# The second scan's end for tokens 512 to 1023, placed behind the first chunk of the ternary feed-forward

## The chip, the cores and the metric

The kernel runs on one core of a Trainium2 chip. The metric is the device time of one execution in microseconds (us). The profile names the core's engines: PE (TensorE: matmuls and transposes), DVE (VectorE), ACT (ScalarE), POOL (GpSimd), and SP (SyncE), whose queue issues most of the transfers (DMAs). Each engine works through its own instructions in order.

## The reference, cut to what matters

Activations `x` are [1024 tokens, 256 features] in float32 (4 sequences of 256). Eight residual blocks follow one another, each on a layer norm of `x`:

```
x += tanh(g) * scan0(ctx, LN(x))        # state-space scan over ctx, gated by silu(LN(x))
x += tanh(g) * mixture0(LN(x))          # 16 experts, top 4, and a shared one
x += tanh(g) * scan1(ctx, LN(x))        # the second scan
x += tanh(g) * ffn1(LN(x))              # ternary weights
x += tanh(g) * attention2(LN(x), ctx)   # 32 heads, rotated keys and queries
x += tanh(g) * ffn2(LN(x))
x += tanh(g) * attention3(LN(x), ctx)
x += tanh(g) * mixture3(LN(x))
```

A scan's state-space part depends on `ctx` alone: `y = scan(ctx) + D*u`. Only its end depends on `x`:

```
y = y * silu(z)        # z = LN(x), x after mixture0
x = x + tanh(g) * y^T
```

The ternary feed-forward is

```
gate, up = split(LN(x) @ Wgu^T)         # 1024 hidden units each
h = silu(gate) * up
x = x + tanh(g) * (h * rsqrt(mean(h*h) + eps)) @ Wp^T
```

It mixes features of one token, never two tokens.

## The kernel before, in words

All of `x` stays in on-chip memory as `x[128, 8 tiles, 256]`. A tile is 128 tokens, and a half `h` is four tiles: half 0 is tokens 0 to 511, half 1 is tokens 512 to 1023. `xn` has the same shape and holds the layer norm that is in use, half by half.

**Order of work.** The kernel is written as a straight program over tiles. A planner then sets each engine's order by readiness and by place in the program; an instruction inside `keep_in_program_order` is kept behind what was written before it for its engine. `pinned_turn` is a PE transpose of that kind, and `silu_z` keeps its two ACT activations that way. The memory of a pool that was closed goes to pools opened later, and their first use waits until the old pool's tiles are done with.

**Second scan and first mixture.** `s1 = Scan(1, ...)` computes the scan's state-space part beside the mixture's blocks (`beside`). The outcome lies in `du` ([128, 2, 1024] float32, 8 KB in each partition), beside `u`, `delta` and others in the pool `ssm1`. When the blocks are done, the mixture's end loads each token's four expert results from DRAM (`y<-y_d`, L969, sixteen transfers of 256 KB through four buffers) and adds them to `x` tile by tile (L981 on DVE; for every third tile ACT L978 and POOL L979). After each tile it calls `hook("done", t)`. After tile 3 and after tile 7, `beside` makes that half's layer norm (stats L179, `rs_r` L186 on POOL, `ln_m` L190, the normed tiles L195 and L198), the gate `silu_z` (L451 on ACT) and `finish`: two DVE products `du<-du,xn` (L459), eight PE transposes in four `yt_ps` tiles (the helper's line, L577), four updates of `x` (L464).

**Ternary feed-forward** (`ffn1`). It makes both halves' layer norms and turns them with `transpose_half2` (eight transposes `xt_ps` a half, L222; high part by ACT L224, rest by DVE L225). Then `chunk(h, c)` runs for two halves of eight chunks of 128 hidden units: eight matmuls into `g_ps` and `u_ps` (L1068), ACT's silu `sg` (L1073), the DVE product `hh` (L1075), its split `hp` (L1077, L1078), its square (L1080 or L1083) and, on POOL, the sum of squares (L1084). `results(h)` multiplies with the second weight matrix (L1104, L1108). [...]the stage takes two as `pt` (tag "tp": `xt_ps` and small things) and six for `g_ps`, `u_ps` and `o_ps`.

**Beside it, the attention's start** (`Heads`, opened just before `ffn1`): it loads `wa` (768 KB, L1168) and `pos` (8 KB, L1173), makes sines and cosines on DVE and ACT (L1177 to L1193), clears `v` on POOL (L1212, L1213), and `first(h, c)` puts the first keys, values and queries between chunks. Its memory is that of the scan's closed pools.

Of the kernel before, what the change touches and what calls it, by code (L numbers as in the profile page):

```python
# [12 lines left out]
F32 = mybir.dt.float32  # L13
# [8 lines left out]
P = 128  # L22
# [3 lines left out]
NT = B * L  # L26
T = NT // P
H2 = 512
# [24 lines left out]
def tile_kernel(ctx: ExitStack, tc: tile.TileContext, a: dict, out: bass.AP):  # L53
# [35 lines left out]
    rows = const.tile([P, 536], F32, name="rows")  # L89
# [80 lines left out]
    def layer_norm_half(h, split=True):  # L170
        for _ in layer_norm_steps(h, nc.vector, nc.scalar, nc.gpsimd, split):
            pass
# [44 lines left out]
    def transpose_half2(pool, h, hi, lo):  # L217

        for k in range(2):
            ps = pool.tile([P, 4, P], F32, name="xt_ps", tag="tp")  # L220
            for i in range(4):
                nc.tensor.transpose(ps[:, i, :], xn[:, h * 4 + i, k * P : (k + 1) * P], ident)  # L222
            pf = ps.rearrange("p i q -> p (i q)")
            nc.scalar.copy(hi[:, k, :], pf)  # L224
            nc.vector.tensor_tensor(lo[:, k, :], pf, hi[:, k, :], ALU.subtract)  # L225
# [5 lines left out]
    class InOrder:  # L231
        def __init__(self, engine):
            self.engine = engine
# [14 lines left out]
    class Scan:  # L248


        def __init__(self, li, es, width, rows, squares, mm):
            self.li, self.mm = li, mm
            self.w, self.wr, self.pr = ssm_w[li], ssm_r[li], ssm_p[li]
            sp = es.enter_context(tc.tile_pool(name=f"ssm{li}", bufs=1))
            self.rot = es.enter_context(tc.tile_pool(name=f"ssm{li}r", bufs=2))
            self.work = es.enter_context(tc.tile_pool(name=f"ssm{li}w", bufs=1))
            dr = es.enter_context(tc.tile_pool(name=f"ssm{li}d", bufs=1, space=bass.MemoryType.DRAM))
            self.width, self.rows, self.squares = width, rows, squares
            self.u = sp.tile([P, 2, NT], F32, name="u")
            self.delta = sp.tile([P, 2, NT], F32, name="delta")  # L260
            self.du = sp.tile([P, 2, NT], F32, name="du")
            self.bcp = sp.tile([96, NT], BF16, name="bcp")
            self.an = sp.tile([P, 2, NS], F32, name="an")
            self.b_dram = dr.tile([NS, NT], F32, name="b_dram")
# [781 lines left out]

    def ffn1(gate, guT, prT, beside):
        with ExitStack() as es:  # L1050
            fp = es.enter_context(tc.tile_pool(name="ffn1", bufs=1))
            fr = es.enter_context(tc.tile_pool(name="ffn1r", bufs=2))
            pt = es.enter_context(tc.tile_pool(name="ffn1t", bufs=2, space=PSUM))
            pg = es.enter_context(tc.tile_pool(name="ffn1g", bufs=2, space=PSUM))
            xps = [[fp.tile([P, 2, H2], F32R, name=f"xp{h}{i}") for i in range(2)] for h in range(2)]
            s2 = [fp.tile([P, H2], F32, name=f"s2{h}") for h in range(2)]
            for h in range(2):
                layer_norm_half(h)
                transpose_half2(pt, h, *xps[h])
            hps, invs = {}, {}  # L1060

            def chunk(h, c):
# [48 lines left out]

            for h in range(2):
                for c in range(8):
                    chunk(h, c)
                    if h == 1 and c == 1:
                        scales(0)
                        results(0)
                    beside(h, c, pt)
# [520 lines left out]
    def g(i):  # L1639
        return tg[:, i : i + 1]  # L1640

    with ExitStack() as es:
        dr = es.enter_context(tc.tile_pool(name="terd", bufs=1, space=bass.MemoryType.DRAM))
        slab_d = [dr.tile([P, 1024], BF16, name=f"slab{i}") for i in range(6)]
# [53 lines left out]
        for h in range(2):  # L1698
            s0.finish(h, g(0), bank, pinned_turn)
        ea.close()  # L1700
        s1 = Scan(1, es, H2, 5, 2, pinned_mm)
        ep = ExitStack()
        kept = {}
        steps = s1.scan(pq, [((dt,), h * H2, H2) for h in range(2) for dt in range(2)], shared=4, c_banks=("c", "c1"), ahead=1)
# [2 lines left out]
        turned = {}  # L1707

        def beside(name, n):
            def step():  # L1710
                if len(made) in (15, 23):
                    widths.append(s1.softplus(len(widths), 1))
                if widths:
                    next(widths[-1], None)
                made.append(next(steps, None))

            if name == "start":
                kept["pre"] = pre = ep.enter_context(tc.tile_pool(name="ssm1pre", bufs=1, side="right"))
                kept["taps"] = s1.taps(pre)
                kept["bc"] = pre.tile([104, NT], F32, name="bc")  # L1720
                s1.decay()
                s1.convolved_by_taps(0, [s1.wide(pq, f"dA{dt}") for dt in range(2)], kept["taps"])
            elif name in ("tables", "pairs"):
                h = int(name == "pairs")
                if h:
                    s1.convolved_by_taps(1, [s1.wide(pq, f"dA{dt}") for dt in range(2)], kept["taps"])
                s1.rows_bc(h, s1.wide(pq, "c"), kept["pre"], kept["bc"])
                for dt in range(2):
                    s1.steps_dt(dt, h, s1.wide(pq, ("y0", "dA1")[dt]), kept["bc"])
                if h:  # L1730
                    s1.ready(pq)
                    ep.close()
                else:
                    for dt in range(2):
                        for _ in s1.softplus(dt, 0):
                            pass
            elif name in ("part", "block"):
                for _ in range(0 if n < 0 else 1 if name == "part" else 2 + (n in (7, 14))):
                    if len(made) < 65:
                        step()  # L1740
            elif name == "branch":
                while len(made) < 65:
                    step()
            elif name == "blocks":
                ew.close()
                tern = et.enter_context(tc.tile_pool(name="wtern", bufs=1, side="right"))
                turned["gu"] = tern.tile([P, 2, 2048], F32R, name="guT")
                turned["pr"] = tern.tile([P, 8, 256], F32R, name="prT")
                yp = es.enter_context(tc.tile_pool(name="moe0y", bufs=1, side="right"))
                ternary_turned(yp, bank, slab_d, turned["gu"], turned["pr"], pinned_turn)  # L1750
                return yp
            elif name == "done" and n % 4 == 3:
                h = n // 4
                layer_norm_half(h)
                s1.silu_z(h)
                s1.finish(h, g(1), bank, pinned_turn)

        mixture(0, g(4), 4, P, weights, route0, weights0, (ph, po, pt), beside, by_tanh=True, G=2)
    eh = ExitStack()
# [3 lines left out]
        heads.bank = lambda shape, dtype, name: pt.tile(shape, dtype, name=name, tag="tp")  # L1763
        heads.first(h, c)

    ffn1(g(5), turned["gu"], turned["pr"], first)
    et.close()
    with tc.tile_pool(name="wfp8", bufs=1, side="right") as w8:
        wq = w8.tile([P, 4608], F32R, name="wq8")
        cols = w8.tile([P, 12], F32, name="cols")  # L1770
        nc.sync.dma_start(out=cols, in_=a["scales2"])
        with tc.tile_pool(name="quant", bufs=1, side="right") as qp:
            xattn2(g(2), heads, Rounding(qp, wq, a["ffn2"]))
        eh.close()
        with tc.tile_pool(name="att3", bufs=1, side="right") as a3:
            attT = a3.tile([P, B, 2, L], F32, name="attT")
            ffn2(g(6), wq, cols, attT)
            xattn3(g(3), attT)
# [106 lines left out]
```

## Time and profile before

| | us |
|---|---|
| median of 3 runs | 979.47 |
| lowest and highest of them | 969.01, 979.48 |
| profiled execution, its own time | 963.2 |
| its span, first to last instruction | 961.5 |
| PE busy | 738.9 (77%) |
| DVE busy | 714.7 (74%) |
| ACT busy | 451.5 (47%) |
| POOL busy | 472.1 (49%) |
| sums of expert results (L981), first start and end of the last | 461.1 to 481.2 |
| first and last matmul of `g_ps` and `u_ps` in the ternary feed-forward, starts | 493.5 to 546.0 |
| its last matmul `o_ps` (L1104), start | 564.0 |

All places in time are counted from the span's first instruction, in the profiled execution. "Busy" leaves out the issuing of transfers. A row such as `DVE x L981 x2` in a chain means two such instructions one after another; in a timeline row, what stands in brackets is how long the engine was idle before it and what ended that. A busy engine in one stage says nothing about another stage, so the text below reads stage by stage. PEclk is PE's granted clock as a share of full speed.

### The profile page before, as it was taken

Reading aid. Unit: us, or ns where it says so; the run is one execution under the profiler, and the core shown is the slowest. Engines: PE = TensorE matmul, PEld = TensorE weight load, DVE = VectorE, ACT = ScalarE, POOL = GpSimd, SP = SyncE. Lnnn points to the kernel's source line nnn. Section 1 sums busy time; section 2 is a strip of 40 time slices with the busy share of each in tenths; the row PEclk is TensorE's granted clock in tenths of the full one; section 3 lists DMA queues with packets and bytes.
Section 4 is the critical chain, followed back from the end, with each engine's and each line's share of the span. In section 5 each row is a group of like instructions: output and inputs, shape, how many; then the busy total and the mean of one; then the engine's idle time right before and its main releaser. Section 6 shows DMA issues by size and latency. Waiting matters only on the chain.

```text
span 961.5 us, 12035 instructions
## 1 busy us (share of the span) xinstructions
PE 738.9 (77%) x3736; PEld 457.3 (48%) x3736; DVE 714.7 (74%) x1406; ACT 451.5 (47%) x875; POOL 472.1 (49%) x432
## 2 busy tenths in 40 slices
PE   5454657669599889896268879989999896989991
PEld 1121222225356555463247756655655675655550
DVE  6998989985989999997787568788775587362332
ACT  4565664513345555353545517666666472102331
POOL 1575685631068878884337524646420332006642
PEclk8586677898679999899579968888869999798996
DMA  4564553301225436573610020000000006603224
GB/s 135 197 231 148 186 179 122 120 1 44 57 78 176 142 117 176 167 177 92 204 34 1 0 99 2 1 2 1 1 2 1 6 1 260 194 4 90 88 67 148
DMA packets 43490, 90.17 MB, mean 94 GB/s; under 512 B 6208, under 2 KB 17360, under 8 KB 43248
## 3 DMA queue, kind: packets, MB, share of 16 engines
q1 hardware_dynamic: 36416, 71.01, 23.2%
q0 software_dynamic: 6144, 16.79, 5.9%
q10 hardware_dynamic: 864, 1.57, 0.4%
q8 instruction: 32, 0.52, 0.2%
q14 instruction: 34, 0.28, 0.1%
HBM read 76.10 MB, written 13.24 MB: 93 GB/s over the span
## 4 chain that ended last, share of the span: by engine, by line
PE 30%; DVE 9%; ACT 4%; DMA 4%; POOL 3%; issue 2%; SPq 0%; DVEq 0%; ACTq 0%; POOLq 0%
PE h_ps L574 5%; PE o_ps L574 3%; PE av_ps L1337 3%; PE sa L1337 2%; DVE gm L239 2%; DMA y<-y_d 2%; PE sb L1337 2%; DMA y_d<-o_sb,place 1%; PE o_ps L1104 1%; DVE m L239 1%; PE o_ps L1558 1%; PE m_ps L1340 1%; PE g_ps L1536 1%; PE h_t_ps L577 1%; PE u_ps L1536 1%
## 5 line engine op out<-in xcount | busy, mean ns | idle before, releaser
L239 DVE TENSOR_TENSOR_SCAN st<-dA,dBu 128x512 f32<-128x512 f32 (+1 forms) x112 | 153.1, 1368 | 4.0 <-ACT dA L239 2.5
L239 POOL TENSOR_TENSOR dBu<-du,b_sb 128x512 f32<-128x512 f32 (+1 forms) x96 | 142.4, 1497 | 20.2 <-DVE st L239 19.2
L239 ACT ACTIVATE dA<-delta,an 128x510 f32<-128x510 f32 (+1 forms) x112 | 83.3, 747 | 126.1 <-DVE st L239 108.2
L239 DVE TENSOR_REDUCE gm<-sa 128x2 f32<-128x512 f32 x128 | 82.0, 683 | 19.8 <-PE sa L1337 19.2
L785 POOL DMA_INDIRECT xg<-xn_d,token x64 | 63.7, 996 | 64.4 <-PE o_ps L574 45.8
L239 DVE TENSOR_TENSOR yc<-st,c 128x512 f32<-128x512 f32 (+1 forms) x112 | 85.6, 764 | 13.0 <-PE c L430 1.7
L430 PE MATMUL c<-bcp,c_selC 96*128 96x512 bf16 x64 | 28.2, 484 | 75.4 <-DVE yc L239 75.3
L239 ACT ACTIVATE ex<-sb 128x512 f32<-128x512 f32 x128 | 69.7, 598 | 34.3 <-PE sb L1337 34.0
L409 PE MATMUL y<-yc,ident 128*128 128x512 f32 x128 | 84.1, 766 | 2.1 <-DVE yc L239 1.2
L871 POOL DMA_INDIRECT y_d<-o_sb,place x64 | 65.9, 1030 | 36.2 <-ACT hT L239 17.0
L409 PEld LDWEIGHTS y<-yc,ident 128*128 128x128 f32 x128 | 31.6, 248 | 88.9 <-issue 70.3
L574 PE MATMUL y<-yc,ident 128*128 128x512 f32 x128 | 68.4, 616 | 2.0 <-DVE yc L239 0.9
L186 POOL TENSOR_TENSOR rs_r<-ln_v,half 128x4 f32<-128x4 f32 x14 | 14.9, 1064 | 100.0 <-DVE ln_v L184 91.0
L1337 PE MATMUL sa<-kT,qT 32*128 32x256 f32 x256 | 42.6, 378 | 8.3 <-DVE gm L239 7.7
L1337 PE MATMUL sb<-qT,kT 32*128 32x256 f32 x256 | 48.2, 363 | 0.1
L1337 PE MATMUL av_ps<-ex,v 128*32 128x256 f32 x512 | 41.8, 445 | 0.6 <-DVE mx L239 0.2
L574 PE MATMUL h_ps<-w0a,xgT 128*128 x160 | 41.5, 406 | 0.7 <-issue 0.7
L239 POOL TENSOR_TENSOR du<-delta,u 128x512 f32<-128x512 f32 x8 | 10.9, 1365 | 63.3 <-DVE delta L239 62.3
L574 PEld LDWEIGHTS y<-yc,ident 128*128 128x128 f32 x128 | 24.8, 196 | 36.1 <-issue 23.0
L1337 PE MATMUL sb<-mxT,onesr 32*128 32x256 f32 x256 | 40.1, 306 | 0.0
L638 ACT ACTIVATE sg<-h_ps 128x176 f32<-128x176 f32 (+1 forms) x30 | 11.2, 374 | 59.2 <-PE h_ps L574 55.4
L639 DVE TENSOR_TENSOR hh<-sg,h_ps 128x176 f32<-128x176 f32 (+1 forms) x44 | 16.5, 376 | 26.3 <-ACT sg L638 16.5
(382 smaller groups left out, 1870.6 us busy)
## 6 DMA issues: line engine op xcount, KB each, us to landing
b_sb<-b_dram SPq DMA_DIRECT2D x32, 512.0 KB
b_sb<-b_dram SPq DMA_DIRECT2D x64, 256.0 KB
w3a<-in_moe3a SPq DMA_DIRECT2D x16, 480.0 KB
w0a<-in_moe0a SPq DMA_DIRECT2D x16, 384.0 KB
y<-y_d SPq DMA_DIRECT2D x24, 256.0 KB
wf<-in_ffn SPq DMA_DIRECT2D x6, 512.0 KB
wf<-in_ffn SPq DMA_DIRECT2D x3, 768.0 KB
xn_d<-xn SPq DMA_DIRECT2D x8, 256.0 KB
```

The costliest lines, as they stand in the source:

```text
L186: pool.tensor_tensor(r, v, half[:, 0:4], ALU.pow)
L239: ins = f(*args, **kw)
L409: self.mm(y_ps[:, q : q + H2], lhsT=ident, rhs=yc[:, q : q + H2], start=(n == 0), stop=(n == NS - 1),)
L430: self.mm(c_ps[:, q : q + H2], lhsT=selC[:, n, :], rhs=self.bcp[:, t0 + q : t0 + q + H2], start=True, stop=True,)
L574: tc.keep_in_program_order(nc.tensor.matmul(*args, **kw))
L577: tc.keep_in_program_order(nc.tensor.transpose(*args))
L638: keep(nc.scalar.activation(sg, g, AF.Silu))
L639: keep(nc.vector.tensor_tensor(out, sg, u, ALU.mult))
L785: nc.gpsimd.indirect_dma_start(out=xgs[b], out_offset=None, in_=xn_d, in_offset=bass.IndirectOffsetOnAxis(ap=token[:, b : b + 1], axis=0),)
L871: ins = nc.gpsimd.indirect_dma_start(out=y_d, out_offset=bass.IndirectOffsetOnAxis(ap=place[:, b : b + 1], axis=0), in_=o_sb[:, j], in_off ...
L1337: tc.keep_in_program_order(nc.tensor.matmul(*args, **kw))
L1536: nc.tensor.matmul(ps, lhsT=wt[:, k, cs], rhs=xp[i][:, k, hs], start=(k == 0 and i == 0), stop=(k == 1 and i == 1),)
```

## The change

Three things change. The end of the second scan for half 1 (`silu_z(1)`, `finish(1)`) leaves the mixture's last hook, where only that half's layer norm stays. `ffn1` makes half 0's layer norm and transposes first, runs chunk (0, 0), then calls `ahead(pt)`, which does the moved end with its transposes in the stage's own two `pt` banks, and after that makes half 1's layer norm and transposes. And `du` of the second scan gets a pool of its own (`ssm1du`, on the right side of memory, opened before everything else there and closed after `ffn1`), since it is now read after the scan's other tiles were closed.

```diff
-        def __init__(self, li, es, width, rows, squares, mm):
+        def __init__(self, li, es, width, rows, squares, mm, du=None):
...
-            self.du = sp.tile([P, 2, NT], F32, name="du")
+            self.du = du or sp.tile([P, 2, NT], F32, name="du")
...
-    def ffn1(gate, guT, prT, beside):
+    def ffn1(gate, guT, prT, beside, ahead):
...
-            for h in range(2):
-                layer_norm_half(h)
-                transpose_half2(pt, h, *xps[h])
+            layer_norm_half(0)
+            transpose_half2(pt, 0, *xps[0])
...
                 for c in range(8):
+                    if (h, c) == (0, 1):
+                        ahead(pt)
+                        layer_norm_half(1)
+                        transpose_half2(pt, 1, *xps[1])
                     chunk(h, c)
...
+    ed = ExitStack()
+    du1 = ed.enter_context(tc.tile_pool(name="ssm1du", bufs=1, side="right")).tile([P, 2, NT], F32, name="du1")
     with ExitStack() as es:
...
-        s1 = Scan(1, es, H2, 5, 2, pinned_mm)
+        s1 = Scan(1, es, H2, 5, 2, pinned_mm, du1)
...
             elif name == "done" and n % 4 == 3:
-                h = n // 4
-                layer_norm_half(h)
-                s1.silu_z(h)
-                s1.finish(h, g(1), bank, pinned_turn)
+                layer_norm_half(n // 4)
+                if n == 3:
+                    s1.silu_z(0)
+                    s1.finish(0, g(1), bank, pinned_turn)
...
+    def second(pt):
+        s1.silu_z(1)
+        s1.finish(1, g(1), lambda shape, dtype, name: pt.tile(shape, dtype, name=name, tag="tp"), pinned_turn)
+
-    ffn1(g(5), turned["gu"], turned["pr"], first)
+    ffn1(g(5), turned["gu"], turned["pr"], first, second)
     et.close()
+    ed.close()
```

## The prediction

> **What bounds the kernel where the change acts.** I read the page first, then the chain of waits from 455 to 500 us, the timeline there, the queue of waits of SP, and the engines' busy time by stage. On the page PE is busy 77% of the span and DVE 74%, but the change touches about a tenth of the span: the first mixture's end (weighted sums, L981), the second scan's end (L459, L577, L464) and the ternary feed-forward (L1068 to L1108). In this stretch the chain runs so:
>
> ```profile
> 455.88 5.09 DMA y<-y_d
> 464.36 3.25 DMA y<-y_d
> 468.40 2.98 DMA y<-y_d
> 484.15 1.03 POOL rs_r L186
> 486.30 1.02 POOL rs_r L186
> 488.56 1.29 DVE du L459 x2
> 489.85 0.09 DVE ln_m L190
> 491.54 0.85 PE yt_ps L577 x4
> 492.40 1.28 PE xt_ps L222 x6
> ```
>
> Columns are start, duration, work. Up to 472 us the loads of expert results (y) set the pace. From 482 to 493.5 us it is a relay through small instructions: the layer norm that feeds the scan's gate (POOL 484.15), the one that feeds the feed-forward's first half (POOL 486.30), and between them, in the way, the scan's two products du and its transposes yt_ps, all for tokens that the feed-forward's first half doesn't need. They stand there because DVE and PE work in order.
>
> **Part 1: the start of the feed-forward, a gain.** The change lets the first half's layer norm pass. Its rs_r ends at 487.32; the Newton steps in the trace of it take until 488.06 (rs_r L152 at 487.90, 0.16 long). Today the next step, ln_m, starts only at 489.77, because du (488.56, 1.29 us for two) is ahead of it. Without du, ln_m is done by 488.2 and the four normed tiles (0.41 each for the two on DVE, 0.60 on ACT, 0.70 on POOL) by 489.0. Today tile 3 is normed at 491.24, behind an x<-yt_ps of the scan's end. Twelve transposes took from 490.86 to 493.68, 0.235 us each; the first four of xt_ps then take 0.94, and ACT's cast of them 0.60 (row xp<-xt_ps: 586/587/598). The first g_ps matmul can start at 489.0 + 0.94 + 0.1 + 0.6 = 490.65 instead of 493.50: 2.85 us.
>
> Here a rule speaks against the sum. The rows of busy time by stage give PE's clock in the column PEclk, behind the busy time and counts of each engine:
>
> ```profile
> 482.00:489.30 7.30, 0.00 (x0) 0.00 (x0) 5.64 (x29) 1.75 (x3) 2.58 (x3) 0.50 0.00 0
> 489.30:493.50 4.20, 3.99 (x17) 3.11 (x17) 3.94 (x12) 1.19 (x2) 1.74 (x2) 0.50 0.09 12
> 493.50:497.00 3.50, 3.50 (x16) 2.86 (x16) 3.12 (x9) 1.28 (x3) 1.67 (x3) 0.98 0.62 213
> ```
>
> PE starts at 489.36 after a pause, and has the full clock only from about 493.6 on. So today the scan's transposes are spent while PE is slow anyhow, and the matmuls find it fast (0.235 us from one to the next, from the chain). The Trainium skill, "TensorE: Matmul & The Clock Gate", Part 1 (the HAM clock gate), says just this: the clock is halved after an idle window, and released by about 3.4 us of activity, not by a count of instructions. After the change PE starts at 489.0 and would have its full clock near 493, at the page's figure or at the 4.2 us seen here. The matmuls from 490.65 to 493 then take 0.47 each: 2.35 us buys 1.17 us of work. By the row of warm matmuls alone the gain is 2.85; by the rule 1.7. I take **-1.7**, since the trace shows the slow stretch too; ends -2.9 and -0.8 (half of it lost to another order of the small instructions).
>
> **Part 2: what moves into the feed-forward.** Every instruction of silu_z(1) and finish(1) is still issued: two ACT activations (1.15), two DVE products (1.29), eight PE transposes, four DVE updates of x (0.91 a pair, 1.82), plus the feed-forward's second layer norm, which already runs beside the first chunks (496.32). On ACT the activations are pinned behind chunk 0's last ACT step; the transposes are pinned behind chunk 0's matmuls on PE, and no DMA is among them. What they meet:
>
> ```profile
> 493.50:504.00 10.50, 9.82 (x46) 7.75 (x46) 9.72 (x34) 6.85 (x13) 3.87 (x5) 0.99 0.22 74
> 504.00:521.50 17.50, 14.08 (x55) 10.53 (x54) 14.86 (x18) 12.88 (x24) 14.19 (x11) 0.90 0.00 0
> ```
>
> PE is busy 23.9 of 28 us, DVE 24.6, ACT 19.7. The eight transposes cost 0.9 at full clock (a pair of xt_ps takes 0.22 at 499.38 and later). PE's 4.1 us of pauses can hide part of that, not all: **+0.5**. DVE is the risk: 24.6 + 3.1 is 27.7 of 28. If nothing leaves DVE, its 3.1 us can show up in full; if Part 3's small trigonometry (fifteen instructions, some 2.5 us at the 0.17 or so of most of them) leaves this stretch, DVE stays as it is. Ends -2.5 and +3.1. The second half's operands are not late: chunk (0,0) starts at 490.65, its Square ends some 5.3 us later as now (493.50 to 498.75), silu, du, four transposes and updates, layer norm and cast need some 12 us more, so 508; the second half's first chunk is at 518 now.
>
> **Part 3: the transfer that the new home of du sets free.** This is the part that the words of the change don't name. du gets a pool of its own beside the scan's other tiles. SP's waits, and its timeline, say what du's old place held back:
>
> ```profile
> SPq L1168 <- DVE du L459: 14.6, 1, 14.6
> SPq L1168 <- PE xt_ps L222: 2.7, 1, 2.7
> 455.88 19.37 SPq L969 DMA_DIRECT2D y<-y_d  x16
> 492.43 0.34 SPq L1168 DMA_DIRECT2D wa<-in_xattn  x1
> 492.82 0.43 SPq L1173 DMA_DIRECT2D pos<-in_pos  x1
> ```
>
> L1168 loads 768 KB of attention weights. It waited 17.3 us for the scan's du products and the transposes that read them, and went out 0.03 us after the last of them had ended (491.34 + 1.06 = 492.40), though it touches neither: its memory is the scan's old memory. In the changed kernel the last user of that memory is the scan's own last step (du<-u, 452.04, 0.75 long), so wa can go out from 452.8 on, and SP sits idle in between the y loads, as each of these waits for a buffer. That is 40 us earlier, in the one stretch where the transfers set the pace (DMA busy 0.92 from 455.9 to 461 at 308 GB/s; 0.84 from 464 to 468). Today wa moves in 2.8 us, from 493.3 to 496.1, with the queue to itself, and hides behind the first chunks.
>
> How much of 2.8 us shows? If SP takes it behind the first four y loads (issued by 457.9), it moves from about 461 to 463.8. The second set's first load is issued at 461.98 now and would move from about 462; it is 1.8 us late, and with it the chain's links at 464.36 and 468.40. If SP takes it before them, all of y is late by 2.8 and by SP's two issues (0.8): +3.6. If it stays behind all y loads, 0. The Trainium skill, "DMA: Bandwidth & Descriptors", Queues, rings and completion order, has each transfer engine take the descriptors of one issuing engine's ring in order; by a fair share of bandwidth y would lose only part, by this rule all that is queued behind. No row here shows both at once; I take the middle place, **+1.8**, ends 0 and +3.6.
>
> The wait's end also frees POOL's memset of v (1.81 and 0.22, idle POOL before 465), the trigonometry and perhaps the first keys. DVE has 8.3 us of idleness ahead of 461, ACT's table is loaded anyhow at 475.80 and Sin needed none of its own at 503.48. Early placement costs nothing there; placed ahead of the sums on DVE it stalls them until pos lands.
>
> **Sum.** -1.7 + 0.5 + 1.8 = +0.6 us on the profiled execution, 963.2 (span 961.5 and 1.7 around it): 963.8. Nothing after 565 us is touched, since the next memory to be handed on is released by the feed-forward's last matmuls in both. The median of the runs shown, 979.47, lies 16 us above the profiled execution, and the runs go from 969.01 to 979.48, so by +0.6 I forecast **980.1 us**: no change that can be told. About 2%, 19.6 us, is what a measurement of this kernel can tell from none; the whole stretch of relays is shorter than that.
>
> **Rivals.** (A) Transfer in the shadow, work ahead of time: wa falls into the pauses (DMA idle a quarter of 461 to 476 us), and trigonometry and first keys run before the feed-forward. Then DVE's stalls go: u_ps waited 2.0 us for hh at 515.95, because a rotation (1.50) and a slowed subtraction (1.75) were ahead of it. -1.7 + 0 - 2.0 = -3.7: 975.8. For it: POOL, ACT and PE idle 455 to 489. Against: POOL's key work (2.77 for one) may sit ahead of rs_r. (B) Slower, at SP's queue: wa and pos ahead of the first y loads. +3.6, and DVE waits for pos with trigonometry ahead of the sums, +2.5; with -1.7 and +0.5 that is +4.9: 984.4. It decides when L1168 is issued before 455.88 . For it: the chain already runs through SP's issues from 452.12 to 455.88. (C) Slower, at PE: the pinned transposes are put right behind chunk 0, while du comes late. Chunk 0's matmuls end near 494, du some 4 us later (Square 495.9, silu 1.15, du 0.65): PE stands 3.7 us. In sum +4.3 : 983.8. It decides if the transposes precede chunk 1's matmuls. (D) The change doesn't do what it says: the first half starts at 493 as before, because the order of the small instructions stays, and Part 3 remains: +2.3, 981.8.
>
> **Chances.** Forecast 0.45, A 0.22, B 0.15, C 0.08, D 0.07, none of these 0.03. All named cases lie within 2%; what lies outside comes from the last and from the spread of runs (963.2 to 979.5 for one kernel). Faster by over 2% 0.03, within 0.93, slower 0.04. The range holds the cases from A to B, and the spread of the runs below: **964 to 987**.
>
> **What would show it.** Right: first g_ps matmul about 2.9 us closer to the last x<-y sum (ends at 481.2 now); PEclk still 0.50 in the first matmuls; yt_ps of the second half at full clock after chunk (0,0); L1168 issued between 455 and 462 and the last sum later by 2 us. Wrong: L1168 at 475 or later (Part 3 falls), PE pauses over 2 us ahead of yt_ps (C), DVE waiting for pos (B), or a difference in stages before 452 us or after 565, where I see no reason for one.

## The result, and the profile after

The changed kernel is slower. Its median is 994.05 us (984.66 to 995.78, 4 runs) against 978.31 for the kernel before, run between them (969.01 to 979.48): 15.7 us, or 1.6%. The ratio is 1.0267, 95% interval [1.0223, 1.031]; it is taken over fast executions alone, those within 1.5% of the fastest of the same kernel, and so need not agree with the ratio of the medians. The profiled execution took 992.51 us (span 990.8; before 963.2 and 961.5).

The table cuts this stretch of each profile into the same pieces. `before_again` and `after_again` are second profiles of the two unchanged kernels; the other names are the experiments told below. **Sums** runs from the first issue of `y` to the end of the last L981, **start** from there to the first `g_ps`, **first** from there to the first `ss_ps`, **rest** to SP's issue of `cols` (L1781 here), **attention** from there to the second load of `wa`. In brackets stands the time at half clock within the attention, from the trace's clock records (in after_warm, **first** ends at the first idle product).

| kernel | sums | start | first | rest | feed-forward | attention |
|---|---|---|---|---|---|---|
| before | 25.3 | 12.3 | 28.2 | 42.6 | 70.8 | 183.7 (58) |
| before_again | 25.4 | 12.3 | 28.8 | 45.0 | 73.9 | 195.6 (92) |
| changed | 26.7 | 11.3 | 33.3 | 47.1 | 80.4 | 195.9 (88) |
| after_again | 29.8 | 11.3 | 33.3 | 47.4 | 80.8 | 183.9 (58) |
| du_alone | 30.3 | 13.1 | 29.1 | 46.2 | 75.3 | 195.8 (89) |
| loads_last | 25.3 | 10.2 | 32.8 | 46.6 | 79.4 | 195.7 (88) |
| loads_last0 | 25.2 | 10.2 | 32.9 | 46.7 | 79.6 | 195.8 (88) |
| after_fill6 | 29.6 | 11.3 | 34.3 | 46.5 | 80.9 | 195.7 (88) |
| after_fill21 | 27.0 | 11.3 | 33.2 | 46.9 | 80.1 | 178.4 (24) |
| before_fill21 | 25.4 | 12.3 | 28.4 | 42.5 | 70.9 | 184.9 (41) |
| keys_late | 30.5 | 11.3 | 27.7 | 48.5 | 76.2 | 181.8 (44) |
| keys_10 | 29.5 | 11.3 | 29.8 | 51.5 | 81.3 | 187.1 (61) |
| after_warm | 29.9 | 11.3 | 33.4 | 46.9 | 80.3 | 184.8 (61) |
| ahead_first | 29.6 | 11.3 | 33.0 | 43.5 | 76.5 | 187.8 (65) |
| after_nosum | 30.1 | 11.3 | 26.9 | 40.7 | 67.6 | 187.9 (55) |
| before_nosum | 25.4 | 12.3 | 22.7 | 36.7 | 59.4 | 185.0 (58) |
| best | 25.5 | 10.1 | 31.8 | 44.5 | 76.3 | 184.9 (41) |

Of the 29.3 us between the spans of the two profiles, 12.2 lie in the attention and 9.6 in the feed-forward. Another 2.3 lie ahead of the first `y` and 4.9 behind the attention. These were not followed up: the first stretch also differs by 2.3 between the two profiles of the kernel before, the second by 4.0 between the two of the changed kernel. SP's timeline of the changed kernel (start, duration, what) shows the early transfer where the prediction put it, behind the first four loads of `y`:

```profile
458.20 2.19 SPq L969 DMA_DIRECT2D y<-y_d  x4
460.60 0.42 SPq L1171 DMA_DIRECT2D wa<-in_xattn  x1
464.48 2.73 SPq L969 DMA_DIRECT2D y<-y_d  x4
467.26 0.46 SPq L1176 DMA_DIRECT2D pos<-in_pos  x1
```

The chain of waits of the changed kernel, from the sums' end to `ss_ps`:

```profile
488.02 1.03 POOL rs_r L186
490.51 0.79 DVE xn L198 x2
491.52 1.02 POOL rs_r L186
493.49 0.87 POOL xn L198
494.40 1.97 PE xt_ps L222 x8
496.37 0.61 PE g_ps L1067
...
501.35 0.53 ACT s L1079
502.43 0.56 DVE du L459
503.04 0.68 DVE du L459
503.72 0.60 DVE hh L1074
504.32 0.79 DVE x L464 x2
...
525.38 1.02 POOL ksl L239
526.40 1.31 issue
527.71 1.72 POOL s L1083
529.48 1.87 PE ss_ps L1089 x8
```

Two things are to be seen. Ahead of the feed-forward, `rs_r` stands twice as before: the other half's layer norm, which the gate needs, is still in front (488.02). Two of its normed tiles (490.51) now stand between the two `rs_r`, which are 3.5 us apart instead of 2.15, and half 0's `rs_r` comes at 491.52, 6.6 us behind the last sum (5.1 before). Then the moved end is on the chain itself: chunk (0, 1)'s `hh` at 503.72 waits in DVE's queue behind the two `du`, which waited for the gate on ACT. At the end of the half POOL's last sum of squares stands behind the attention's keys (`ksl`), and `ss_ps` waits for it.

Busy time by stage, in three profiles: before, before_again, changed. Behind the stretch and its length stand busy time and count of PE, PEld (PE's weight loads), DVE, ACT and POOL, then PEclk, the DMA share and GB/s.

```profile
493.50:521.70 28.20, 24.11 (x100) 18.49 (x100) 24.78 (x51) 19.73 (x37) 18.06 (x16) 0.94 0.08 28
521.70:564.30 42.60, 37.87 (x239) 33.24 (x237) 21.30 (x52) 16.49 (x30) 18.98 (x16) 0.92 0.00 1
```

```profile
495.90:524.70 28.80, 24.71 (x101) 18.96 (x101) 25.00 (x51) 19.72 (x37) 18.03 (x16) 0.91 0.08 27
524.70:569.73 45.03, 40.17 (x238) 35.65 (x237) 22.34 (x51) 16.46 (x30) 18.23 (x16) 0.86 0.00 1
```

```profile
490.00:496.20 6.20, 1.80 (x9) 1.58 (x9) 2.78 (x14) 1.79 (x3) 2.56 (x3) 0.50 0.00 0
496.20:499.70 3.50, 3.50 (x9) 2.71 (x9) 1.35 (x2) 1.18 (x2) 0.00 (x0) 0.50 0.00 0
499.70:529.50 29.80, 22.99 (x112) 18.00 (x110) 24.36 (x43) 18.46 (x35) 16.79 (x14) 0.96 0.00 1
529.50:576.60 47.10, 39.55 (x226) 35.15 (x226) 22.62 (x52) 17.35 (x32) 19.11 (x16) 0.85 0.00 1
```

PE is busy 66.0 us in the changed feed-forward and idle 14.3; in before it is busy 62.0 and idle 8.8, in before_again 64.9 and 9.0. So 5.4 to 5.5 us more are waiting, whichever profile of the kernel before is taken. The rest, 4.1 or 1.1 us, is PE being busy longer, where the clock plays a part: it is at half speed for 20.6 us of the feed-forward, against 10.4 in before and 17.2 in before_again. The kernel before alone differs by 3.1 us here, so a part of the 9.6 us depends on which of its executions was profiled.

### The profile page after: what moved, and what is told of

The parts are those of the page before. It is cut to its first block, busy times and chain, and to the rows that moved or that the text cites. A ratio compares the mean times of both kernels' runs of the same rounds, so it can differ in the third digit from the quotient of the medians.

```text
span 990.8 us, 12026 instructions
## 1 busy us (share of the span) xinstructions
PE 759.0 (77%) x3736; PEld 470.3 (47%) x3736; DVE 717.1 (72%) x1406; ACT 451.1 (46%) x875; POOL 472.7 (48%) x432
## 4 chain that ended last, share of the span: by engine, by line
PE 32%; DVE 9%; POOL 4%; DMA 4%; ACT 3%; issue 2%; SPq 0%; DVEq 0%; POOLq 0%; ACTq 0%
PE h_ps L574 5%; PE av_ps L1340 3%; PE o_ps L574 3%; PE sa L1340 2%; DMA y<-y_d 2%; DVE gm L239 2%; PE sb L1340 2%; PE o_ps L1103 1%; DMA y_d<-o_sb,place 1%; PE g_ps L1539 1%; PE o_ps L1561 1%; PE u_ps L1539 1%; DVE m L239 1%; PE out_ps L1340 1%; PE m_ps L1343 1%
## 5 line engine op out<-in xcount | busy, mean ns | idle before, releaser
L1340 PE MATMUL sb<-qT,kT 32*128 32x256 f32 x256 | 50.9, 384 | 0.0
L1340 PE MATMUL av_ps<-ex,v 128*32 128x256 f32 x512 | 45.3, 479 | 0.4 <-DVE mx L239 0.2
L1340 PE MATMUL sb<-mxT,onesr 32*128 32x256 f32 x256 | 42.6, 322 | 0.0
L574 PE MATMUL h_ps<-w3a,xgT 128*128 x96 | 35.9, 500 | 1.2 <-DVE xgT L802 1.2
```

Of the source, the lines that this page charges most:

```text
L574: tc.keep_in_program_order(nc.tensor.matmul(*args, **kw))
L1340: tc.keep_in_program_order(nc.tensor.matmul(*args, **kw))
```

## The experiments

Three theories stood against each other: the moved end itself (1), the early transfer (2), and PE's clock in the attention (3). Each run's time is a median, its ratio is to the kernel before on the same chip.

### The transfer: du_alone, loads_last, loads_last0

du_alone is the kernel before with only these lines of the change:

```diff
-            self.du = sp.tile([P, 2, NT], F32, name="du")
+            self.du = du or sp.tile([P, 2, NT], F32, name="du")
...
-        s1 = Scan(1, es, H2, 5, 2, pinned_mm)
+        s1 = Scan(1, es, H2, 5, 2, pinned_mm, du1)
```

> The kernel before, with only du in a pool of its own: nothing of the scan's end is moved, and the load of wa is free early, as in the changed kernel. Theory 1 (the moved end is what costs: its layer norm stands in the middle of the chunks, POOL's sums of squares come late, PE pauses and its clock falls): this kernel has none of that. Sums of the expert results about 1.4 us longer (26.7 instead of 25.3), first half of the feed-forward (first g_ps to first ss_ps) at 28 us, its rest at 43; median 978 to 981 us, ratio to before 1.000 to 1.003. Theory 2 (the early transfer and what follows from it is the cost): first half at 31 us or more, ratio 1.012 or more. Theory 3 (most of the 29 us is where PE's clock windows fall in the attention): the attention's length follows its half-clock time, here as in every other run, about half a us for each us at half clock, whatever the edit.

981.21 us, ratio 1.0141 [1.0093, 1.019]. The ratio meets theory 2's mark (1.012 or more), not theory 1's (up to 1.003); the feed-forward's first half, 29.1 us, is nearer to theory 1's 28 than to theory 2's 31. The whole feed-forward stays near the kernel before (75.3; 70.8 and 73.9 there), so the move is what lengthens most of it. But the sums took 30.3 us instead of the 26.7 expected, the start 13.1. Thus the transfer's side effect was mis-sized, even though it is not the main cost in the feed-forward. Against before_again, whose attention is as long, this profile is 7.3 us longer: 5.7 in the sums and the start, 1.4 in the feed-forward.

loads_last and loads_last0 are the changed kernel with the transfers held behind `y`. loads_last held the last mixture's loads and stores in order too:

```diff
-            nc.sync.dma_start(out=wa, in_=a["xattn2"])
+            tc.keep_in_program_order(nc.sync.dma_start(out=wa, in_=a["xattn2"]))
...
-                    nc.sync.dma_start(
-                        out=ys[k],
...
+                    tc.keep_in_program_order(nc.sync.dma_start(
+                        out=ys[k],
```

> The changed kernel with the loads of wa and pos held in program order behind all loads of y; the scan's end stays moved, and the twenty or so small products of the angles on DVE now come behind the layer norm. Theory 1: the sums go back to about 25.3 us, and nothing else comes back: first half of the feed-forward 32 us or more, PE waiting over 2.5 us for the sum of squares ahead of ss_ps; median 989 to 993, ratio to before 1.012 to 1.026. Theory 2: near the kernel before, 976 to 981, ratio 0.998 to 1.004. Theory 3: says nothing of this edit; the attention's length follows its half-clock time.

992.21 us, ratio 1.0242 [1.0187, 1.0298]. The sums went back to 25.3 us and the feed-forward stayed at 79.4, as theory 1 has it. The time says little, since the last mixture's end took 24 us instead of 16 by my own edit. loads_last0 pins `y` in the first mixture alone:

> The changed kernel with the loads of wa and pos held behind the loads of y, now in the first mixture alone (in the run before, the last mixture's loads and stores had been put in order as well, and its end took 24 us instead of 16). Theory 1: sums 25.3 us, first half of the feed-forward 32 to 33.3, its rest 46 to 48, last mixture 158 to 164; 1 to 3 us faster than the changed kernel at equal clock in the attention. Theory 2: first half of the feed-forward below 30, 6 us faster or more.

983.22 us, ratio 1.0142 [1.0098, 1.0186]; sums 25.2, start 10.2, feed-forward 79.6. Theory 2 falls for the feed-forward. For the sums it holds, and the start is 1.1 us shorter too: the two `rs_r` (489.37 and 491.52) are 2.15 us apart again, with no normed tile between them. On this chip after_again's median was 992.95, so holding the loads gives back 9.7 us, where 1 to 3 were expected at equal clock in the attention; 7.0 of them stand in the sums, the start and the feed-forward of the two profiles. By whole time, then, the early transfer without the move (1.0141) and the move without the early transfer (1.0142) cost about the same, and each about half of the 1.0267 of both.

Why do the sums lose 1.4 us in one profile and 4.5 in another of the same kernel? POOL's and DVE's timelines of after_again, 478 to 482 us:

```profile
478.32 3.84 POOL L979 TENSOR_TENSOR x<-x,y 128x256 f32<-128x256 f32 x1
```

```profile
478.30 2.06 DVE L981 SCALAR_TENSOR_TENSOR x<-y,gws,x 128x256 f32<-128x256 f32 x5
480.28 1.28 DVE L459 TENSOR_TENSOR du<-du,xn 128x512 f32<-128x512 f32 x2
```

One POOL sum takes 3.84 us instead of some 0.8, just while DVE works through seven instructions with two operands each. A buffer of `y` comes free that much later, and the next load with it. The profiles with the early transfer have this stretch in all but two (sums 29.5 to 30.5), and the two without it have 26.7 and 27.0. In those two the same sum starts just before DVE's L1191, a small product of the angles, and takes 0.8 us, and it is L1191 that takes 0.71 us instead of 0.38. In loads_last0, with the loads held, no such sum is over 0.8:

```profile
478.10 1.54 POOL L979 TENSOR_TENSOR x<-x,y 128x256 f32<-128x256 f32 x2
```

The Trainium skill, "GPSIMD Engine Reference", 8 (Key points), says that POOL shares its SBUF interfaces with DVE and contends with DVE instructions of two SBUF inputs; these rows agree. That it is the cause of the stretch was not tried by itself.

### The attention's clock: before_again, after_again, after_fill6, after_fill21, before_fill21

> The kernel before, unchanged, profiled a second time. Theory 3: the median of before lies 15 us above its profiled execution because the attention's end or another long stretch is at half clock in most executions; if this one is near 978, the attention (first profile 183.7 us with 58 us at half clock) should be 190 us or more with 70 us or more at half clock, and the feed-forward's two parts again 28 and 43 us. If the clock isn't the cause, the attention stays within 1 us of 183.7 at whatever total.

980.12 us: the unchanged kernel took 195.6 us for its attention, with 92 us at half clock. In the attention both kernels have the same instructions in the same order on DVE, ACT and POOL, and on PE but for some records that are missing or swapped, as they also are between two profiles of one kernel. Its last part, from 136 us behind the issue of `cols`, in four profiles, each by its own name (before, before_again, changed, after_again):

```profile
700.30:748.00 47.70, 43.48 (x422) 27.02 (x422) 29.31 (x86) 27.86 (x58) 3.48 (x4) 0.86 0.01 2
```

```profile
705.70:765.30 59.60, 56.02 (x423) 34.31 (x422) 29.62 (x87) 28.24 (x59) 3.65 (x5) 0.60 0.01 1
```

```profile
712.60:772.50 59.90, 56.30 (x427) 34.55 (x424) 29.91 (x88) 28.36 (x59) 3.85 (x5) 0.60 0.01 1
```

```profile
715.00:762.90 47.90, 43.70 (x427) 27.18 (x423) 29.54 (x87) 27.75 (x59) 3.61 (x5) 0.86 0.01 2
```

Nearly equal counts, nearly equal DVE and ACT; PE's clock is 0.86 or 0.60, and 12 us hang on it. Each kernel shows both. The rest of before_again's feed-forward took 45.0 us where 43 was expected, with 12.2 us at half clock instead of 6.8.

> The changed kernel, unchanged, on the same chip as the three beside it. In the six profiles so far the attention took 182 to 184 us with 44 to 58 us at half clock, or 195.6 to 195.9 with 88 to 92, and the unchanged kernel has shown both. Counted from the issue of cols, the 3.413 us grid of the clock's windows lay 1.04 and 2.0 us later in the two short ones, 1.33 to 1.62 in the four long ones. Theory 3 in its sharp form (the attention's length is set by where it starts on that grid, and the changed kernel starts it at an unlucky place most of the time): attention 195.7 again in most runs, ratio to before 1.022 to 1.031. In its loose form (each execution draws afresh, whatever the kernel): ratio to before anything from 1.01 to 1.03, with as many short runs as long ones.

992.95 us, ratio 1.0265 [1.0232, 1.0299]. Six of seven executions took 991.6 to 995.7 us; the profiled one took 978.92 and has the short attention. The 13 executions of the kernel before beside it were all at 963.7 to 974.7. By their times, then, the changed kernel had the long attention far more often (only the profiled executions show it directly). On another chip the kernel before had 38 of 68 executions between 974 and 981 us, 30 between 954 and 969 and none between: there, again by time, it was long in more than half of them. So the change may tip the share, but isn't alone in that; what sets the share stays open.

Does the attention's start on the clock's grid decide? Two fillers, pinned in front of its first product (N = 6 and 21):

```diff
+            fill = pm.tile([P, 256], F32, name="fill_ps", tag="mm")
+            for i in range(N):
+                mm(fill, lhsT=identr, rhs=kTs[0][:, 0, :], start=True, stop=True)
             mxTs, exs, gms = {}, {}, {}
```

> The changed kernel with six idle products of 256 columns on PE (0.14 us each at full clock, some 0.85 us) in front of the attention's first product: it only starts the attention later. Sharp form of theory 3: the grid lies at 0.6 to 0.8 us behind the issue of cols, off the unlucky places, attention near 184.6 instead of 195.9, and the kernel 8 to 11 us faster than the changed one in spite of the added work. Loose form: 0 to 1 us slower than the changed kernel, with the same share of long attentions. Theories 1 and 2: 0.8 us slower.

988.43 us, ratio 1.0181 [1.0136, 1.0226], long attention in the profile (195.7). The sharp form got no test: six products ran in the 0.58 us in which PE waited anyway, and the first product of the attention started 0.60 us behind `cols` instead of 0.55.

> The same with 21 such products, some 2.95 us. Sharp form of theory 3: the grid lies at about 2.0 us (1.55 less 2.95 plus 3.41), as in the kernel with the late keys, whose attention took 181.8; so attention 185 to 187 with the filler in it, and 6 to 9 us faster than the changed kernel. Loose form, and theories 1 and 2: 2 to 3 us slower than the changed kernel.

976.98 us, ratio 1.0088 [1.0052, 1.0123]: 16 us less than after_again, though 21 products were added and the attention's first product came 1.9 us later. All eight executions lie between 972.1 and 980.0. The clock records show what is different: the full clock ahead of the attention lasts 10.2 us instead of 6.8, one more window, and the windows that follow fall otherwise. The last part:

```profile
713.50:755.90 42.40, 38.56 (x413) 24.79 (x406) 27.61 (x82) 25.92 (x55) 2.71 (x3) 0.98 0.01 2
```

The grid lay at 1.56 us behind `cols`, near the 1.62 of the changed kernel, while the attention's first product stood 1.9 us later on it. So the place that I had named (2.0) was not reached. Whether the filler worked by keeping PE busy, or by the other place that it gave the attention's start, these runs don't tell apart.

> The kernel before with the 21 idle products in front of the attention's first product, which in the changed kernel took 16 us off the median in spite of 2 us of added delay: PE's clock kept one more window at full speed there, and the attention took 178.4 us with 24 us at half clock. If that is a property of the attention's start and not of the change: attention 178 to 179 here as well, in every run; 2 to 6 us faster than the kernel before where that has mostly short attentions (183.9), ratio 0.993 to 0.998. If the filler only shifts: 2 us slower, ratio 1.002.

964.62 us, ratio 0.9938 [0.9899, 0.9977]. The attention took 184.9 us and not 178 to 179. All 14 executions lie between 960.5 and 967.1, where 38 of the 68 of the kernel before beside it were above 974. That is the whole gain: beside the 30 others, whose median is 962.8, this version is 1.8 us slower, as the filler that only shifts would be. It pays where the kernel before is often long (median 974.59 here) and not where it is short; the ratio lies between these two readings. The sharp form stays open: in the profiles without filler the grid lay at 1.04, 1.30, 2.00 and 2.14 us behind `cols` in four with 182 to 185 us, at 1.33 to 1.62 in all with 195.6 and more; but keys_10 at 1.56 took 187.1, after_nosum at 1.00 took 187.9, and at 2.47 and 2.49 ahead_first took 187.8 and before_nosum 185.0.

### The feed-forward: keys_late, keys_10, after_warm, ahead_first, after_nosum, before_nosum

keys_late moves the attention's first keys (in keys_10 the line reads `h == 1 and c == 0`):

```diff
-            if h == 0 and c == 4:
+            if h == 1 and c == 2:
                 for _ in self.keys(0):
```

> The changed kernel with the first keys of the attention (k_ps, four products r on POOL, two sums on DVE, one cast on ACT and a subtraction on POOL) placed behind the second half's third chunk instead of the first half's fifth. Theory 1 with POOL's queue as the carrier (four r and one ksl, 7.4 us, stand ahead of the last sums of squares): ss_ps no longer waits over 1.5 us, first half of the feed-forward 29.5 to 30.5 us instead of 33.3, no stretch of 10 us at half clock behind it, the rest 43 to 45 instead of 47.1; 5 to 7 us less than the changed kernel, 986 to 989. Rival within theory 1 (the relay alone delays the chunks; ACT and DVE are behind, not POOL): first half 32 us or more, less than 2 us gained. Theory 3: the attention's length follows its half-clock time.

974.79 us, ratio 1.0138 [1.0093, 1.0183]. The first half fell to 27.7 us, but the rest rose to 48.5: 4.2 us less in all, below the 5 to 7 expected. The attention, 181.8 us in this profile instead of 195.9, gives the greater part of the shorter time. PE's waits in the feed-forward (in all, times, longest), the changed kernel, then keys_late:

```profile
PE ss_ps L1089 <- POOL s L1083: 5.7, 2, 3.4
PE xt_ps L1293 <- POOL xn L198: 2.5, 1, 2.5
```

```profile
PE ss_ps L1089 <- POOL s L1083: 3.0, 2, 2.3
PE xt_ps L1293 <- POOL xn L198: 2.9, 1, 2.9
PE t_ps L1245 <- POOL ksl L239: 1.2, 1, 1.2
```

> The changed kernel with the attention's first keys placed behind the second half's first chunk instead of the first half's fifth. With the late keys (behind the third chunk) ss_ps waited 0.65 us instead of 3.4 and the clock stayed up, but xn on POOL then stood behind the keys and PE waited 2.9 us for it: the cost was moved on. Here POOL takes the keys between the last sum of squares of the first half and the next layer norm. Theory 1 with POOL's queue as carrier: first half of the feed-forward 27.5 to 29, rest 43 to 46, together 71.5 to 75 against 80.6 in the changed kernel, no 10 us at half clock behind ss_ps. Rival (the two layer norms' relay costs by itself, wherever the keys stand): together 78 or more.

984.99 us, ratio 1.0181 [1.0141, 1.0222]; feed-forward 81.3, as without the edit. The wait has a new name:

```profile
PE o_ps L1103 <- DVE x L1107: 5.4, 1, 5.4
```

`o_ps` needs a bank that the update L1107 frees, and this waits for a scale whose `rs_r` now stands behind the keys on POOL. In both placements, what stood behind the keys on POOL waited. The expectation of 71.5 to 75 fell; the rival's 78 or more was met.

after_warm puts 22 idle products in front of `ss_ps`:

```diff
-                ss = pt.tile([P, 4], F32, name="ss_ps", tag="tp")
+                ss = pt.tile([P, H2], F32, name="ss_ps", tag="tp")
+                for i in range(22 if h == 0 else 0):
+                    pinned_mm(
+                        ss[:, 256:512], lhsT=guT[:, 0, 0:P], rhs=hps[0, 7][1][:, 0:256], start=True, stop=True
+                    )
+                ss = ss[:, 0:4]
```

> The changed kernel with 22 idle products on PE (256 columns, 0.14 us each at full clock, some 3.1 us) right in front of ss_ps, where PE waits 3.4 us for POOL's last sum of squares. The wait itself stays. If the pause is what lets the clock fall (part of theory 1): first half 33 to 34 as in the changed kernel, but results(0) at full clock, the 10 us at half clock behind it gone, rest 42.5 to 45 instead of 47.1: 2 to 5 us less in the feed-forward. If the fall has another cause, the rest stays at 46.5 to 48.

983.30 us, ratio 1.0096 [1.0044, 1.0148]; feed-forward 80.3. Inconclusive: the products read the last `hp` and PE waited 2.4 us for it, so they ran where `ss_ps` would have run, and moved it from 33.3 to 37.2 us. From `ss_ps` on the rest took 43.1 us instead of 47.4, which is about what the filler had cost.

ahead_first changes one line of the changed kernel:

```diff
-                    if (h, c) == (0, 1):
+                    if (h, c) == (0, 0):
```

> The changed kernel with the moved end and the second layer norm put ahead of chunk (0, 0) in the program instead of behind it, so that du, yt_ps and the norm go into the queues beside chunk 0. The early transfer stays. Theory 1: the relay is some 4 us earlier on all queues, and the sums of squares with it: first half 29 to 31, PE's wait ahead of ss_ps below 2 us. If the place makes no difference to POOL: 33 as before.

983.17 us, ratio 1.0113 [1.007, 1.0156]. The wait at the first `ss_ps` falls from 3.4 to 0.8 us, as expected, and the wait for `xn` in the rest is gone; the rest takes 43.5 us, near the kernel before. The first half stays at 33.0, where 29 to 31 were expected: there the chunks meet the moved end even earlier (2.2 us for `xn`, 1.2 for `sg`).

The last two leave out the fourteen POOL additions of squares, in both kernels; the scale comes from the first chunk's squares alone.

```diff
-                    nc.gpsimd.tensor_tensor(s2[h], s2[h], sq, ALU.add)
```

> The changed kernel without the fourteen additions on POOL that sum the squares of the chunks (the scale is then taken from the first chunk's squares alone): it leaves out 14 times 1.3 us on POOL, the last of which ss_ps waited for. Theory 1, POOL's queue as the carrier: first half 28.5 to 30, no wait of PE for s or for xn over 1 us, feed-forward together 71 to 75 instead of 80.6. Rival (the relay through DVE, ACT and PE): 77 or more.

> The kernel before without the same fourteen additions. There PE waited 2.2 us in all for the sums. Theory 1: feed-forward 68 to 71 instead of 70.8 to 73.8, so that the gap between the two kernels in this stage falls from 7 to 10 us to 5 or less. Rival: the gap stays at 7 us or more.

970.37 us, ratio 1.0010 [0.9944, 1.0077], and 955.82, ratio 0.9900 [0.9846, 0.9953]. Busy time by stage, before_nosum, then after_nosum:

```profile
496.20:518.90 22.70, 22.09 (x98) 17.47 (x98) 19.71 (x50) 18.13 (x35) 7.77 (x9) 0.99 0.10 34
518.90:555.60 36.70, 34.06 (x229) 30.10 (x227) 22.34 (x52) 16.91 (x32) 10.28 (x9) 1.00 0.00 1
```

```profile
500.30:527.10 26.80, 25.80 (x119) 21.05 (x119) 19.91 (x43) 18.44 (x34) 5.87 (x7) 0.93 0.00 1
527.10:567.90 40.80, 35.16 (x215) 31.14 (x214) 24.14 (x53) 17.21 (x32) 11.12 (x10) 0.92 0.00 1
```

Both feed-forwards lose over 11 us and end below every figure that had been expected. The gap between them stays at 8.2 us (67.6 against 59.4), the rival's mark. So POOL's sums are not the carrier of the whole gap, and theory 1 in that form falls. They carry a part: without them PE's waiting differs by 3.4 us (6.6 against 3.2) instead of 5.5. The other 4.8 us are PE being busy longer, with 10.6 us at half clock against 0.4. The starts of `hh` on DVE, counted from the first `g_ps`, tell where the gap grows:

| chunk's `hh` | before | before_again | du_alone | changed | changed less before | before_nosum | after_nosum | gap |
|---|---|---|---|---|---|---|---|---|
| first | 2.9 | 2.8 | 3.8 | 3.8 | 1.0 | 3.0 | 3.9 | 0.9 |
| second | 4.6 | 4.6 | 6.1 | 7.4 | 2.9 | 4.6 | 7.5 | 3.0 |
| eighth | 24.6 | 24.6 | 25.8 | 28.0 | 3.4 | 20.9 | 24.3 | 3.3 |
| twelfth | 42.0 | 45.1 | 46.3 | 50.4 | 8.4 | 36.9 | 42.9 | 6.0 |
| last | 54.9 | 57.9 | 59.2 | 64.2 | 9.3 | 48.9 | 55.8 | 6.9 |

1.0 us is there at the first `hh`, where the matmuls run at half clock, and 1.9 more come at the second, where `du` stands in front of `hh`, with or without sums. du_alone, without the moved end, has 1.5 of these 2.9. The next 5.1 (2.7 without the sums) come around results(0) and the attention's layer norm: PE's wait for the late sum is 1.2 us longer than before, `o_ps` then runs at half clock, and the twelfth `hh` stands in DVE's queue behind that norm's `rs_q`, which waits for POOL. But 3.1 of the 5.1 are there in before_again as well, where nothing is moved and PE waits for that sum as short as in before (2.2 us): there too the clock is at half for 10.2 us, and in before for 3.4. So 2.0 are left that only the move shows. How these divide was not measured one by one.

### The parts together: best

The moved end ahead of chunk (0, 0), the loads held, and the 21 products.

> The moved end and second layer norm ahead of chunk (0, 0), the loads of wa and pos held behind those of y, and the 21 idle products in front of the attention. From the parts: sums 25.3 and start 10.2 as with the loads held, feed-forward 76.5 as with the moved end first, attention 178 to 185; the kernel before with the filler alone had 25.4, 12.3, 70.9, 184.9. So the moved end still loses 3 to 4 us: 966 to 970 where that one had 964.6; ratio to before 0.996 to 1.002. If the earlier start carries through: 962 or less.

972.90 us, ratio 1.0059 [1.0014, 1.0104]: above the 966 to 970 expected, though the parts of the profile came as expected (25.5, 10.1, 76.3, 184.9). Against before_fill21 the earlier start of 2.2 us doesn't make up for 5.4 us in the feed-forward. No version of the move tried here pays.

## Why the prediction was wrong

The profile of before and that of after_again both have the short attention, so their stages can be set against the sum: 963.2 and 978.92 us, a difference of 15.7, which is by chance also that of the first medians. By stage, rounded, it is +1.2 ahead of the first `y`, where nothing is moved that the sum priced, +4.5 in the sums, -1.0 in the start, +10.0 in the feed-forward, +1.1 behind it. The prediction had +0.6.

**Part 2 is the step that failed first**: +0.5 forecast, upper end +3.1, while the feed-forward grew by 10.0 us (6.5 between the two profiles with the long attention). 1.5 of this belongs to Part 1 (the slow first matmuls, below), so 8.5 or 5.0 are left. Part 2 priced the moved instructions as busy time that PE's pauses or DVE's slack must hold, and it let the pauses hide most of PE's share. The pauses grew instead: PE waits 5.4 to 5.9 us more. What the sum lacked is the place in the queues. The gap that opens by the second chunk, where DVE carries the moved `du`, stays open through the half, and the keys, sums and norms on POOL come later or in another order: PE waits for the last sum of squares 3.4 us instead of 2.2, and for the attention's `xn` 2.5 us where there was no such wait. Part 2 also took no account of PE's clock, which was at half speed for 20.6 us of this stage, against 10.4 or 17.2. The sentence that the second half's operands are not late was right in its own terms (needed at 518, made by 516) and beside the point, since it was the first half's chunks that were late.

**Part 3** named the right mechanism at the right instruction (L1171 at 460.60). In the two profiles without the stretched POOL sum the sums grew by 1.4 to 1.7 us, where +1.8 was forecast. Mis-sized was the rest: with POOL's sum stretched to 3.8 us the sums lost 4.1 to 5.2 in all the others, above the upper end of 3.6. The forecast priced the transfer alone and not another arrangement of POOL and DVE beside it. By whole time this part weighs as much as the move: du_alone, which has nothing else of the change, has a ratio of 1.0141.

**Part 1** looks nearly right and isn't. It put the first `g_ps` 2.85 us closer to the last sum and took 1.17 off for slow matmuls. Measured, the first `g_ps` came 1.0 us closer, and PE stayed at half clock for 3.5 us behind it: the ninth matmul starts 3.55 us behind the first instead of 2.03 (9 matmuls in 496.20:499.70, 16 in the prediction's 493.50:497.00). So 1.5 us went there, and the part came to +0.5 instead of -1.7. With the loads held it came to -2.15 and +1.1, so -1.1. That the matmuls would be slow was right, as the rule on the clock gate had it. What failed is that the sum kept half 0's `rs_r` at 5.1 us behind the last sum; with the early transfer two tiles of the other half's norm stand in front of it, and it comes at 6.6.

**"Nothing after 565 us is touched"** held for the instructions and not for the time. Twelve us can come or go there by PE's clock in one and the same kernel; by their times, six of seven executions of the changed kernel had them where none of 13 of the kernel before had. Ahead of the first `y` and behind the attention, another 7.2 us of the difference between the profiles of before and changed were not followed up. The Trainium skill, "TensorE: Matmul & The Clock Gate", Part 1, gives the window as 3413 ns, which the lengths of the clock records show too (multiples of 3.413 us), and for modeling takes the ramp to full clock as under 1% of a typical kernel's span. 1% of this kernel is 9.6 us; the traces have 11.9 us between two executions of the unchanged kernel's attention alone, where the clock falls and rises many times, and the measurement decides.

Of the rivals, none came as written. C was tested by its own mark: PE did not stand ahead of `yt_ps` for the moved end. B needed L1171 ahead of the first `y`. D expected the start unchanged; it came 1.0 us closer. A expected PE's stall at `u_ps` behind `hh` to go; it only shrank from 2.5 to 1.6 us.

## What to carry to other kernels

Work that stands in a stage where PE is idle and at half clock may cost little there: here, taking it out shortened the start by 1.0 us, or 2.15 with the loads held, and the next matmuls gave back 1.5 or 1.1 of this at half clock. Before moving it into a stage whose chunks already pass through four in-order queues, price the queue position at every later meeting, not only its busy time. When a buffer moves, ask which transfer its old place held back, and what stands beside the new place of that transfer. Before a difference of one per cent is explained, profile the unchanged kernel twice: here its own attention differed by 12 us. A few idle products ahead of a long stage can change how PE's clock runs through it: here, by their times, none of 22 executions of two kernels with 21 such products had the long attention, and they cost some 2 us where the attention was already short.

## What was not expected of the hardware

- POOL's adds slow DVE as well as being slowed by it. Without the fourteen additions, DVE's busy time in the first half of the kernel before's feed-forward fell from 24.78 us for 51 instructions to 19.71 for 50. Its subtraction `hp` took 0.91 us instead of 1.10 and a rotation's sum `ro` 0.64 instead of 1.16, while `hh`, which reads one operand from PSUM, stayed at 0.68. The whole feed-forward fell by 11.4 us (14.5 against before_again), though PE had waited only 2.2 us for the sums; a part of that is PE's clock, at half speed for 0.4 us there instead of 10.4.
- One POOL addition was held for 3.84 us across seven DVE instructions, not across one.
- The same 422 to 427 matmuls of the attention's end ran at a clock of 0.86 or 0.60; with 2.7 us of idle products some 136 us earlier, 413 of the changed kernel's ran at 0.98.
